# Eleven expert units beside the state space block: side chains at its two ends, list planning inside them, routing decisions in pairs, D on the matrix engine

## The chip, the cores and the metric

The kernel runs on one core of a Trainium2 chip. The metric is the device time of one execution in microseconds (us), the median over several runs. A profile is one further execution, recorded by the hardware profiler; its own time and its span are given below. The engines are TensorE (PE; PEld is its weight load), VectorE (DVE), ScalarE (ACT), GpSimd (POOL) and SyncE (SP, which here only issues DMAs). A line such as L961 is line 961 of the kernel before.

## The reference: what is computed

There are 4096 tokens of 256 float32 values. Three blocks stand one after the other, each with a residual:

```python
x = x + 0.5 * moe(layernorm(x))            # MoE1
x = x + attn(layernorm(x))                 # state space block and a small MLP
x = x + 0.5 * moe(layernorm(x))            # MoE2, the same weights as MoE1

def attn(x):
    x = x + mamba(rmsnorm(x))
    h = square(relu(rmsnorm(x) @ c_fc.T))
    return x + h @ c_proj.T

def mamba(xn):                             # 2 sequences of 2048 tokens
    x_in, z = split(xn @ in_proj.T)        # 512 channels each
    u = silu(causal_conv4(x_in))
    dt_low, B, C = split(u @ x_proj.T)     # 64, 16 and 16 columns
    dt = softplus(dt_low @ dt_proj.T + bias)
    h[t] = h[t-1] * exp(dt[t] * A) + dt[t] * u[t] * B[t]    # 512 channels x 16 states
    y[t] = sum_over_states(h[t] * C[t])
    return ((y + u * D) * silu(z)) @ out_proj.T
```

`moe` picks two of eight experts for each token. Each expert is 256 -> 1024 -> 256 with a ReLU. A token's place in an expert's list is the number of earlier tokens with the same choice; there is a capacity of 1280 places for each choice and expert, and a token beyond it is dropped. So the places of a token depend on the tokens before it and on none after it.

## The kernel before, in words

**Routing.** Tokens are handled in tiles of 128. `route` (L303) normalises a group of n tiles, multiplies with the gate weights, and decides (L374 to L453, many small VectorE operations): the two experts, the gates, and by a running count each token's place in the lists. Then it writes the token numbers into the list tile with a few products against one-hot matrices (`one`, `eqb`, L466, L468, and `ll` on PE, L480 to L488). The normalised rows with their two gates go to the DRAM table `rows`.

**Plan and units.** `store_list` (L495) transposes the list and stores it to DRAM. `plan` (L504) cuts each expert's list into units of 256 places and works out, for all 39 units that could be needed, which list entries a unit takes and which expert's weights. `units` (L570) runs 32 of them: for each unit POOL gathers by indirect DMA two times 128 token numbers (`ids`, L589), the rows (`xb`, L600) and, if the expert changes, its weights (`w`, L609, 2.18 MB); PE transposes the rows (L621), multiplies into the hidden layer (`hp`, L640), ACT adds the bias and takes the ReLU (L645), PE multiplies back (`yp`, L656), VectorE adds the bias and scales by the gate (L660, L661), and POOL scatters with addition into `acc` or `out` (L662). The order is written out by hand: ids five units ahead, rows and weights three ahead. Units past 32 are in a branch that is entered only if the plan needs them. `moe1` (L697) routes all 32 tiles in five groups and then runs its units; `moe2` (L726) finds its routing done by the block before it. Both load three sets of the first expert's weights by SP (L567) beforehand.

**The state space block.** `mamba` (L1095) works on eight chunks of 512 tokens. `recurrence` (L928) has 512 slots: chunk, pair of channel blocks, state, block of the pair. In a slot ACT makes `dA` (L969), POOL `db` (L961; one operation for both blocks of the pair, 128x1024, three tiles in rotation), VectorE the scan `h` (L979) and the product with `ct` (L989), ACT keeps the last state (`st`, L984), and PE sums the products over the states into `y_ps` (L994). SP loads `bt` and `ct`, one row of B and C spread over 128 partitions, one pair ahead into three tiles each. After a pair's 16 states `gate` (L996) adds D times the convolved input (VectorE, L1002) and multiplies by silu(z) (POOL, L1006).

Everything else is a side chain, a generator that yields before each step what the step needs: `chunk_front` (L735: load of `acc`, norms, projections, convolution, dt), `log1p` (L870), `gates` (L893: silu(z)), `chunk_tail` (L1026: output projection, MLP, store of x, and `route` on the chunk's four tiles for MoE2). `Side` (L70) is the planner that interleaves them when the program is built: it counts each engine's use in microseconds (OWN is what a slot takes of each engine) and issues a step when the engines that it needs are no further ahead than BEHIND and its input is not later than EARLY. `until` forces a chain to a mark. What cannot be placed in a slot waits; before the first scan and after the last one the chains run on their own. The engines execute in the order of issue.

Of the kernel before, what the change touches and what calls it, by code (L numbers as in the profile page):

```python
# [17 lines left out]
P = 128  # L18
# [17 lines left out]
NU = K2 * NT // UN  # L36
MU = NU + E - 1
NWB = 3
W_2 = ND * FF
W_B1 = W_2 + NF * D  # L40
W_B2 = W_B1 + NF
# [9 lines left out]
XB = 4  # L51
PR = 2
NP = NC // PR
GROUPS = (4, 4, 8, 8, 8)
# [3 lines left out]
class Need:  # L58
# [4 lines left out]
    def __init__(self, pe=0.0, act=0.0, dve=0.0, pool=0.0, bank=0, free=0, after=None, sets=None):  # L63
        us = {"pe": pe, "act": act, "dve": dve, "pool": pool}
        self.us = {e: t for e, t in us.items() if t}
        self.bank, self.free, self.sets = int(bank), free, sets
        self.after = None if after is None or after[1] < 0 else after


class Side:  # L70
# [6 lines left out]
    OWN = {"dve": 1.8, "act": 0.88, "pe": 0.88, "pool": 1.25}  # L77
# [9 lines left out]
    def begin(self, chain, at=0.0):  # L87
        self.chains.append([chain, None, at])
        self.advance(self.chains[-1])
# [9 lines left out]
    def advance(self, chain):  # L99
        need = next(chain[0], None)  # L100
        while need is not None and not isinstance(need, Need):
            self.begin(need, chain[2])
            need = next(chain[0], None)
        chain[1] = need
        if need is None:
            self.chains.remove(chain)

# [9 lines left out]
    def step(self, chain):  # L117
# [8 lines left out]
        if need.sets:  # L126
            self.mark(need.sets, end)
# [27 lines left out]
    def until(self, mark):  # L155

        while mark[1] >= 0 and mark not in self.marks:
            self.step(min(filter(self.may, self.chains), key=lambda c: self.start(c)[1]))


class Kernel:
# [6 lines left out]
    def setup(self):  # L168
        nc, ins = self.nc, self.ins
        cp = self.ctx.enter_context(self.tc.tile_pool(name="const", bufs=1))  # L170
        self.cpool = self.ctx.enter_context(self.tc.tile_pool(name="count", bufs=2))
        dp = self.ctx.enter_context(self.tc.tile_pool(name="scratch", bufs=1, space=DRAM))
# [32 lines left out]
        self.need = const([P, K2 * CAP // UN], "need")  # L205
        nc.gpsimd.iota(self.need, pattern=[[UN, K2 * CAP // UN]], base=0, channel_multiplier=0,
# [29 lines left out]
        none = const([1, 1], "none_i", I32)  # L236
        nc.gpsimd.memset(none, NT)

# [24 lines left out]
        for c in range(NC):  # L263
            for k in range(DC):
                nc.vector.tensor_scalar_mul(
                    self.taps[:, c, k, :], self.ident, self.half[:, c, k : k + 1]
                )
        self.minus = const([P, 1], "minus")
# [12 lines left out]
        self.rows = dp.tile([NT + 1, RW], F32, tag="rows", name="rows")  # L281
        row = const([1, RW], "none")
        nc.gpsimd.memset(row, 0.0)
        nc.sync.dma_start(out=self.rows[NT:, :], in_=row)
        self.lists = [dp.tile([NULL + 1, 1], I32, tag=f"list{i}", name="lists") for i in range(2)]
        for t in self.lists:
            nc.sync.dma_start(out=t[NULL:, :], in_=none)
# [15 lines left out]
    def route(self, x, t0, pool, bank):  # L303

        nc = self.nc
        n = x.shape[1]
        W, W3, Q = [P, n, E], [P, n, K2], K2 * E
        num = self.exp_m8.unsqueeze(1).to_broadcast(W)

        def t(name, shape=W, dtype=F32, **kw):  # L310
            return pool.tile(shape, dtype, tag=f"r_{name}", name=name, **kw)
# [25 lines left out]
        lg = t("lg")  # L337
        for j0 in range(0, n, 4):
# [22 lines left out]
            for j in range(4):  # L361
# [5 lines left out]
                lg[:, j0 : j0 + 4, :], lq, self.gb.unsqueeze(1).to_broadcast([P, 4, E]), ALU.add  # L367
            )

# [50 lines left out]
        g1 = row[:, :, D]  # L420
        nc.vector.scalar_tensor_tensor(g1, e2, 0.5, rden, ALU.mult, ALU.mult)
        nc.vector.scalar_tensor_tensor(row[:, :, D + 1], rden, 0.5, g1, ALU.mult, ALU.subtract)
# [30 lines left out]
        nc.vector.tensor_tensor(at, at, late, ALU.add)  # L453
        yield Need(dve=1.6)

        WO, WN = [P, n, K2, P], [P, n, K2, E * PB]
# [20 lines left out]
        ll = psum("ll", [P, K2, 2, E * PB])  # L477
# [12 lines left out]
        nc.sync.dma_start(out=self.tiles(self.rows[:NT, :], n)[t0 // n], in_=row)  # L490
# [4 lines left out]
    def store_list(self, pool, ps, to):  # L495

        nc, n = self.nc, K2 * E * PB
        lp = ps.tile([P, P], F32, tag="lists", name="lists")[:n, :]
        nc.tensor.transpose(lp, self.list.rearrange("p c b -> p (c b)"), self.ident)
        lt = pool.tile([P, P], I32, tag="p_list", name="lt")[:n, :]  # L500
        nc.vector.tensor_copy(lt, lp)
        nc.sync.dma_start(out=to[:NULL, :].rearrange("(b p) o -> b (p o)", p=P), in_=lt)

    def plan(self, pool):  # L504

        nc = self.nc
        v = nc.vector
        WE, WB = [P, MU, E], [P, MU, UB]  # L510
        nn = K2 * CAP // UN

        def t(name, shape, dtype=F32):
            return pool.tile(shape, dtype, tag=f"p_{name}", name=name)

        kept, ks = t("kept", [P, K2 * E]), t("ks", [P, E])
        v.tensor_scalar_min(kept, self.count, float(CAP))
        k0 = kept[:, :E]
        v.tensor_tensor(ks, k0, kept[:, E:], ALU.add)
        more, nu, cu, cx = t("more", [P, E, nn]), t("nu", [P, E]), t("cu", [P, E]), t("cx", [P, E])  # L520
        v.tensor_tensor(
            more, ks.unsqueeze(2).to_broadcast([P, E, nn]),
            self.need.unsqueeze(1).to_broadcast([P, E, nn]), ALU.is_gt,
        )
        v.tensor_reduce(nu, more, AX.X, ALU.add)
        v.tensor_tensor_scan(cu, self.ones[:, :E], nu, 0.0, ALU.mult, ALU.add)
        v.tensor_tensor(cx, cu, nu, ALU.subtract)
        past, inn = t("past", WE), t("inn", WE)
        un = self.unum.unsqueeze(2).to_broadcast(WE)
        v.tensor_tensor(past, un, cu.unsqueeze(1).to_broadcast(WE), ALU.is_ge)  # L530
        v.tensor_tensor(inn, un, cx.unsqueeze(1).to_broadcast(WE), ALU.is_ge)
        v.tensor_tensor(inn, inn, past, ALU.subtract)
        eu = t("eu", [P, MU])
        v.tensor_reduce(eu, past, AX.X, ALU.add)

        def of_unit(name, values):
            m, r = t("m", WE), t(name, [P, MU])
            v.tensor_tensor(m, inn, values.unsqueeze(1).to_broadcast(WE), ALU.mult)
            v.tensor_reduce(r, m, AX.X, ALU.add)
            return r.unsqueeze(2).to_broadcast(WB)  # L540

        k0u, ksu, cxu = of_unit("k0u", k0), of_unit("ksu", ks), of_unit("cxu", cx)
        euu = eu.unsqueeze(2).to_broadcast(WB)
        r, m0, m1 = t("r", WB), t("m0", WB), t("m1", WB)
        v.scalar_tensor_tensor(r, cxu, -float(UN), self.upos, ALU.mult, ALU.add)
        v.tensor_tensor(m0, r, k0u, ALU.is_lt)
        v.tensor_tensor(m1, r, ksu, ALU.is_lt)
        at, a1, a0, idx = t("at", WB), t("a1", WB), t("a0", WB), t("idx", WB, I32)
        v.scalar_tensor_tensor(at, euu, float(CAP), r, ALU.mult, ALU.add)
        v.tensor_tensor(at, at, k0u, ALU.subtract)  # L550
        v.scalar_tensor_tensor(a1, at, float(NSLOT - NULL), m1, ALU.add, ALU.mult)
        v.scalar_tensor_tensor(a0, k0u, -float(NSLOT), m0, ALU.add, ALU.mult)
        v.scalar_tensor_tensor(idx, a1, float(NULL), a0, ALU.add, ALU.add)
        same, at2, widx = t("same", [P, MU]), t("at2", [P, MU]), t("widx", [P, MU], I32)
        v.tensor_scalar(same[:, :NWB], eu[:, :NWB], 0.0, None, ALU.is_equal)
        v.tensor_tensor(same[:, NWB:], eu[:, NWB:], eu[:, : MU - NWB], ALU.is_equal)
        v.scalar_tensor_tensor(at2, eu, float(P), self.part, ALU.mult, ALU.add)
        v.scalar_tensor_tensor(widx, same, SKIP, at2, ALU.mult, ALU.add)
        nunits = t("nunits", [1, 1], I32)
        v.tensor_copy(nunits, cu[0:1, E - 1 : E])  # L560
        return idx, m0, widx, nunits

    def first_expert(self, pool):

        w = [pool.tile([P, WW], F32, tag=f"w{i}", name=f"w{i}") for i in range(NWB)]
        for t in w:
            self.nc.sync.dma_start(out=t, in_=self.ins["expert"][:P, :])  # L567
        return w

    def units(self, lo, hi, todo, w, lists, acc, pool, ps):  # L570

        nc = self.nc
        idx, m0, widx, _ = todo
        ids, xb, xT, gate = {}, {}, {}, {}

        def params(u):
            wu = w[u % NWB]
            return (
                wu[:, :W_2].rearrange("p (k f) -> p k f", k=ND),
                wu[:, W_2:W_B1].rearrange("p (f d) -> p f d", f=NF),  # L580
                wu[:, W_B1:W_B2], wu[:, W_B2:],
            )

        def fetch_ids(u):
            if u >= hi:
                return
            ids[u] = pool.tile([P, UB], I32, tag="ids", name="ids", bufs=8)
            for j in range(UB):
                nc.gpsimd.indirect_dma_start(  # L589
# [597 lines left out]
```

## Time and profile before

| | |
|---|---|
| time, median of three runs | 2442.43 us (2440.75 to 2444.05) |
| profiled execution: its own time, its span | 2459.16 us, 2457.4 us |
| busy share of the span | PE 83%, DVE 56%, ACT 42%, POOL 59% |
| first unit's first matmul L640, MoE1 and MoE2 | at 117.9 and 1983.4 us |
| last matmul of MoE1 | at 584.1 us |
| first scan, end of the last scan | at 667.4 and 1893.2 us |
| one bt load, one rows store, median | 3.6 us, 6.5 us |

The profile's page gives the busy time of each engine, the span in slices, the costliest groups of instructions and the DMA issues. A group's row has its line, engine, operation, what it writes and reads, its number, its busy time, the mean ns of one, and the idle time just before it with what ended that. A row of waits names who waited for whom, the sum in us, how often, and the longest. The windows view gives each engine's busy time in a stretch, PE's granted clock as a share of full speed, the DMA engines' busy share and GB/s.

### The profile page before, as it was taken

Reading aid. Unit: us, or ns where it says so; the run is one execution under the profiler, and the core shown is the slowest. Engines: PE = TensorE matmul, PEld = TensorE weight load, DVE = VectorE, ACT = ScalarE, POOL = GpSimd, SP = SyncE. Lnnn points to the kernel's source line nnn. Section 1 sums busy time; section 2 is a strip of 40 time slices with the busy share of each in tenths; the row PEclk is TensorE's granted clock in tenths of the full one; section 3 lists DMA queues with packets and bytes.
Section 4 is the critical chain, followed back from the end, with each engine's and each line's share of the span. In section 5 each row is a group of like instructions: output and inputs, shape, how many; then the busy total and the mean of one; then the engine's idle time right before and its main releaser. Section 6 shows DMA issues by size and latency. Waiting matters only on the chain. (4 is left out here: it accounts for less than half of the span.)

```text
span 2457.4 us, 23707 instructions
## 1 busy us (share of the span) xinstructions
PE 2051.3 (83%) x7196; PEld 1296.4 (53%) x7196; DVE 1386.9 (56%) x2358; ACT 1029.3 (42%) x2307; POOL 1441.5 (59%) x1145
## 2 busy tenths in 40 slices
PE   3499999997687977979889698798686469999998
PEld 1288888885232433424334243243232258888887
DVE  5611111111298989989999899899998301111111
ACT  3122222222467675665756557557343212222222
POOL 2355555642478776675866767668554155556553
PEclk7699999998799988989989899798787779999999
DMA  8145454461133433334434334334342225454463
GB/s 312 62 139 143 117 172 113 114 180 18 57 123 127 121 120 110 121 96 130 142 100 129 102 121 137 94 121 120 111 127 75 108 82 168 121 146 125 131 183 97
DMA packets 141791, 302.00 MB, mean 123 GB/s; under 512 B 24447, under 2 KB 65174, under 8 KB 135638
## 3 DMA queue, kind: packets, MB, share of 16 engines
q1 hardware_dynamic: 103766, 176.50, 23.0%
q0 software_dynamic: 37888, 123.88, 18.2%
q8 instruction: 62, 1.02, 0.2%
q14 instruction: 75, 0.61, 0.1%
HBM read 318.85 MB, written 34.23 MB: 144 GB/s over the span
## 5 line engine op out<-in xcount | busy, mean ns | idle before, releaser
L994 PE MATMUL y_ps<-hc,ident 128*128 128x512 f32 x1024 | 588.8, 676 | 212.3 <-DVE hc L989 200.3
L961 POOL TENSOR_TENSOR db<-dtu,bt 128x1024 f32<-128x1024 f32 x256 | 601.7, 2358 | 207.1 <-DVE h L979 173.8
L645 ACT ACTIVATE h<-hp,w 128x256 f32<-128x256 f32 x512 | 215.0, 471 | 779.3 <-issue 501.7
L979 DVE TENSOR_TENSOR_SCAN h<-dA,st,db 128x512 f32<-128x512 f32 x384 | 494.6, 1288 | 32.3 <-ACT dA L969 3.8
L656 PE MATMUL yp<-w,h 128*128 128x256 f32 x2048 | 457.4, 382 | 10.1 <-issue 10.1
L994 PEld LDWEIGHTS y_ps<-hc,ident 128*128 128x128 f32 x1024 | 184.1, 202 | 531.9 <-DVE hc L989 399.9
L640 PE MATMUL hp<-xbT,w 128*128 128x256 f32 x2048 | 457.5, 382 | 1.6 <-DVE xbT L625 1.6
L640 PEld LDWEIGHTS hp<-xbT,w 128*128 128x128 f32 x2048 | 392.4, 192 | 56.6 <-DVE xbT L625 2.4
L656 PEld LDWEIGHTS yp<-w,h 128*128 128x128 f32 x2048 | 387.1, 192 | 61.7 <-issue 10.9
L969 ACT ACTIVATE dA<-dt,A 128x512 f32<-128x512 f32 x512 | 357.4, 699 | 0.3
L989 DVE TENSOR_TENSOR hc<-h,ct 128x512 f32<-128x512 f32 x512 | 345.1, 674 | 4.7 <-ACT st L984 4.7
L625 DVE COPY xbT<-tp 128x512 f32<-128x512 f32 x64 | 44.3, 692 | 463.6 <-PE tp L621 383.9
L984 ACT COPY st<-h 128x1 f32<-128x1 f32 x512 | 80.7, 158 | 402.9 <-DVE h L979 401.1
L660 DVE TENSOR_TENSOR y<-yp,w 128x256 f32<-128x256 f32 x128 | 54.4, 425 | 340.9 <-PE yp L656 340.9
L662 POOL DMA_INDIRECT acc<-y,ids x64 | 102.5, 1602 | 165.6 <-PE hp L640 76.9
L662 POOL DMA_INDIRECT out<-y,ids x64 | 102.2, 1597 | 165.5 <-DVE y L661 72.1
L979 DVE TENSOR_TENSOR_SCAN h<-dA,db 128x512 f32<-128x512 f32 x128 | 157.1, 1228 | 31.6 <-POOL db L961 17.9
L589 POOL DMA_INDIRECT ids<-lists,idx x128 | 128.5, 1004 | 70.8 <-issue 70.8
L600 POOL DMA_INDIRECT xb<-rows,ids x128 | 130.7, 1021 | 39.0 <-issue 39.0
L909 PE MATMUL in_ps<-rT,w_in 128*128 128x512 f32 x256 | 127.6, 624 | 7.0 <-ACT xpad L794 5.6
L801 PE MATMUL cv_ps<-xpad,taps 128*128 128x512 f32 x256 | 122.2, 603 | 0.1
L909 PEld LDWEIGHTS in_ps<-rT,w_in 128*128 128x128 f32 x256 | 50.2, 200 | 72.9 <-issue 48.1
(199 smaller groups left out, 1944.8 us busy)
## 6 DMA issues: line engine op xcount, KB each, us to landing
bt<-bc SPq DMA_DIRECT2D x256, 256.0 KB, 3.6
ct<-bc SPq DMA_DIRECT2D x256, 256.0 KB, 3.4
w<-in_expert SPq DMA_DIRECT2D x6, 2180.0 KB, 12.8
rows<-row SPq DMA_DIRECT2D x10, 516.0 KB, 6.5
x<-in_x SPq DMA_DIRECT2D x8, 512.0 KB, 8.8
acc<-x SPq DMA_DIRECT2D x8, 512.0 KB, 7.6
x<-acc SPq DMA_DIRECT2D x8, 512.0 KB, 4.9
out<-x SPq DMA_DIRECT2D x8, 512.0 KB, 3.6
```

Of the source, the lines that this page charges most:

```text
L589: nc.gpsimd.indirect_dma_start(out=ids[u][:, j : j + 1], out_offset=None, in_=lists[:, :], in_offset=bass.IndirectOffsetOnAxis(ap=idx[:, u ...
L600: nc.gpsimd.indirect_dma_start(out=xb[u][:, j, :], out_offset=None, in_=self.rows[:, :], in_offset=bass.IndirectOffsetOnAxis(ap=ids[u][:, ...
L640: nc.tensor.matmul(hp[:, q, :], lhsT=w1[:, k, (f + q) * P : (f + q + 1) * P], rhs=xT[u][:, k, :], start=(k == 0), stop=(k == ND - 1),)
L645: nc.scalar.activation(h[:, f + q, :], hp[:, q, :], AF.Relu, bias=b1[:, f + q : f + q + 1])
L656: nc.tensor.matmul(yp, lhsT=h[:, f, j * P : (j + 1) * P], rhs=w2[:, f, :], start=(f == 0), stop=(f == NF - 1),)
L662: nc.gpsimd.indirect_dma_start(out=acc[:, :], out_offset=bass.IndirectOffsetOnAxis(ap=ids[u][:, j : j + 1], axis=0), in_=y[:, j, :], in_of ...
L909: self.nc.tensor.matmul(mp, lhsT=self.w_in[:, k, m * P : (m + 1) * P], rhs=rT[:, k, :], start=(k == 0), stop=(k == ND - 1),)
L961: nc.gpsimd.tensor_tensor(db[n], chunks[i]["dtu"][c // PR], bt[n].unsqueeze(1).to_broadcast(WP), ALU.mult)
L969: nc.scalar.activation(dA[k], chunks[i]["dt"][c], AF.Exp, scale=self.A[:, c, s : s + 1])
L979: nc.vector.tensor_tensor_scan(h[k], dA.pop(k), db[k // PR][:, k % PR, :], chunks[i - 1]["state"][:, c, s : s + 1] if i % (T // TC) else 0 ...
L989: nc.vector.tensor_tensor(hc, h.pop(k), ct[k // PR], ALU.mult)
L994: nc.tensor.matmul(y[c], lhsT=self.ident, rhs=hc, start=(s == 0), stop=(s == DS - 1))
```

## The change

- **Units moved.** MoE1's loop runs 28 units (NU_A). Its plan cuts each expert's list twice, into units that hold tokens of the first half of the sequence and, after all of those, units of the second half alone. The last four (NU_B) run inside `mamba`, in a side chain `beside`, at slots -96, -64, -32 and 0; the load of chunk 4 waits for them. After chunk 3 a plan of the first half of MoE2's lists is made in the chain (`plan_half`); seven full units (NU_C) from it run from slot 448 on. `plan_rest` plans what is left, in the chain after the last chunk, and begins its ids and rows. MoE2's loop runs 25 units (NU_D).
- **Their data.** The expert weights are two tensors (W1 and b1; W2 and b2), gathered separately. The side units have one tile for each (`wa`, `wb`). Rows of the first four chunks go to two tables. SP loads one set of first weights instead of three.
- **Decisions in pairs.** In the block `route` only makes logits and stores rows for an even chunk; the odd one decides for eight tiles at once. Lists are still written per chunk.
- **D on PE.** The accumulation of `y_ps` starts with a matmul of the convolved input by a diagonal matrix `skip`. `gate` is one VectorE product.
- **Buffers.** To make room: `bt` and `ct` 3 -> 2, `db` one tile of 128x512 per slot (4, made three slots ahead), `zs` and `dt` 6 -> 4, `dtu` 3 -> 2, `xc` 8 -> 6, `x` 4 -> 1 (loaded again as `xt` for the tail), `hc` 4 -> 5. The planner's OWN for VectorE is 1.95 instead of 1.8; chains get ranks.

The core of the diff:

```diff
+NU_A, NU_B, NU_C, NU_D = 28, 4, 7, 25
...
-    OWN = {"dve": 1.8, "act": 0.88, "pe": 0.88, "pool": 1.25}
+    OWN = {"dve": 1.95, "act": 0.88, "pe": 0.0, "pool": 1.27}
...
+    def spread_units(self, feed, m0, acc, last, pool, name, slots, known):
...
+        for u, slot in enumerate(slots):
+            yield Need(after=("slot", slot))
+            if u == 0:
+                yield from turn(0)
...
+            for f in range(0, NF, 2):
+                lone = self.lone
+                yield Need(pe=1.8, bank=not lone, after=at("wa", u))
...
+                self.into_hidden(hp, f, w1, xT[u])
...
+            for j in range(UB):
+                yield Need(pe=3.6, bank=j == 0 and not lone, after=at("wb", u))
...
+                self.from_hidden(yp[:, j, :], j, w2, h)
...
+            yield put(u, y)
+            if u + 1 < n:
+                yield Need(pool=1.0, sets=(name + "wb", u + 1), late=9.0)
+                feed.params_of(u + 1, wb)
...
-        def drive(n):
-            if n < len(pairs):
...
-                db[n] = sp.tile(WP, F32, tag="db", name="db", bufs=3)
-                nc.gpsimd.tensor_tensor(
-                    db[n], chunks[i]["dtu"][c // PR], bt[n].unsqueeze(1).to_broadcast(WP), ALU.mult
-                )
+        def drive(k):
+            if k < len(order):
...
+                db[k] = sp.tile(W1, F32, tag="db", name="db", bufs=4)
+                nc.gpsimd.tensor_tensor(db[k], chunks[i]["dtu"][c // PR][:, q, :], bt[n], ALU.mult)
...
             if s == 0:
                 y[c] = pools["yps"].tile(W1, F32, tag="y", name="y_ps")
-            nc.tensor.matmul(y[c], lhsT=self.ident, rhs=hc, start=(s == 0), stop=(s == DS - 1))
+                nc.tensor.matmul(
+                    y[c], lhsT=self.skip[:, c, :], rhs=chunks[i]["xc"][c], start=True, stop=False
+                )
...
+            nc.tensor.matmul(y[c], lhsT=self.ident, rhs=hc.pop(k), start=False, stop=(s == DS - 1))
...
-            nc.vector.scalar_tensor_tensor(
-                yc, ch["xc"][c], self.chan[:, c, DC + 1 : DC + 2], y[c], ALU.mult, ALU.add
-            )
             side.until(("z", NC * i + c))
-            nc.gpsimd.tensor_tensor(yc, yc, ch["zs"][c], ALU.mult)
+            nc.vector.tensor_tensor(yc, y[c], ch["zs"][c], ALU.mult)
...
+        if i % 2 == 0:
+            self.pair = {}
+        yield from self.route(x, i * NJ, pool, lambda tag: (ps, "mm"), to, self.pair)
         yield Need(sets=("routed", i))
+        if i == NCHUNK // 2 - 1:
+            yield self.plan_half(pools["exp"])
+        if i == NCHUNK - 1:
+            yield from self.plan_rest(pools)
...
+    def beside(self, pools):
+
+        chunk = NC * DS
+        slots = [chunk * (u - 3) // 2 for u in range(NU_B)]
...
+        slots = [chunk * (NCHUNK - 1) + 16 * u for u in range(NU_C)]
```

## The prediction, made before the result was known

> **What bounds the kernel now.** I began with the busy shares on the page and the costliest groups, then cut the span into its stages by the windows view, then read the waits inside each stage. The windows give core 0's stretch, its length, and the busy time of each engine, PE's clock, DMA share and GB/s:
>
> ```profile
> 142.30:584.10 441.80, 441.77 (x2106) 388.67 (x2104) 76.81 (x214) 104.13 (x248) 241.61 (x201) 1.00 0.49 136
> 584.10:667.40 83.30, 45.27 (x96) 18.52 (x96) 9.65 (x26) 29.06 (x49) 22.40 (x41) 0.77 0.11 33
> 667.40:1893.20 1225.80, 1003.10 (x2426) 428.20 (x2426) 1126.36 (x1499) 737.48 (x1648) 858.21 (x591) 0.91 0.39 118
> 1893.20:1990.00 96.80, 43.47 (x146) 26.84 (x146) 23.22 (x87) 17.68 (x39) 22.61 (x25) 0.70 0.23 87
> 1990.00:2457.40 467.40, 453.17 (x2152) 398.16 (x2150) 79.53 (x221) 105.81 (x252) 251.80 (x211) 0.99 0.48 135
> ```
>
> Both expert loops are PE from end to end (441.77 of 441.80). The timeline shows one unit every 14.25 us there. The recurrence between them is VectorE: 1126 of 1226 us, PE 82%. Two open ends, 83 us before the first scan and 97 us after the last, have every engine half idle or worse: a chain of small steps. So PE work taken out of a loop is worth its whole time, and costs less at the ends than it weighs, but there it stands in line with the chain's own matmuls.
>
> VectorE's groups inside the recurrence:
>
> ```profile
> L979 DVE TENSOR_TENSOR_SCAN h<-dA,st,db 128x512 f32<-128x512 f32 x384 | 494.6, 1288 | 32.3 <-ACT dA L969 3.8 <-ACT st L984 0.5 <-DVE hc L989 0.5
> L989 DVE TENSOR_TENSOR hc<-h,ct 128x512 f32<-128x512 f32 x510 | 343.8, 674 | 4.7 <-ACT st L984 4.7
> L1002 DVE SCALAR_TENSOR_TENSOR yc<-xc,chan,y_ps 128x512 f32<-128x512 f32 x30 | 22.1, 736 | 1.2 <-PE y_ps L994 1.2
> L385 DVE SCALAR_TENSOR_TENSOR key<-oh,key 128x32 f32<-128x32 bf16 x7 | 7.6, 1089 | 0.0
> L374 DVE TENSOR_REDUCE top<-lg 128x4 f32<-128x32 f32 x7 | 1.3, 184 | 0.2
> ```
>
> A slot (scan 1.29, product 0.67) is 1.99 us with its gap, 1.92 where no state comes in: 128 x 1.925 + 384 x 1.99 = 1011 us. The other 215 are side work and waits. The last two rows are route's: on 128x32 one operation takes 184 ns and another 1089, so operations are the price, not elements. All rows of the decision (L374 to L453) sum to 81.4 us over seven chunks, 11.6 each.
>
> **Part by part**, against the profiled execution's span of 2457.4 us (its own time 2459.16; the median shown is 2442.43, so 0.7% lies between; I carry the difference over unchanged).
>
> *Start of MoE1.* Three weight loads stand in SP's queue ahead of the first row store, and the routing of the second group stands behind that store:
>
> ```profile
> DVE lg L366 <- PE lq L362: 22.4, 4, 15.8
> ```
>
> One load is left there: 2.18 MB of 6.54 that took 21 us is 7 us, so about 14 go (bounds 0 and 15.8). The plan grows: 7.9 us of VectorE now; 39 units x 16 half-expert columns instead of 8, and eight quantities of 39 x 64 elements, each one product and one sum of about 2.6 us: 19.4, +11.5 (bounds +5 and +16). Net **-2.5**, bounds -10 and +10.
>
> *MoE1 loop.* 31 further units become 27: 4 x 14.25 = **-57**. Two weight gathers a unit instead of one add about 1.3 us of POOL, which is busy 242 of 442; without that cover PE would wait 7 us for a late set.
>
> *First open end.* Two units and half a hidden layer are placed there, some 2.3 x 14.25 = 33 us of PE, among 45 us of the chain's own, in 83.3 us. 38 are free; the steps alternate (projection, taps, gate, projection), so a batch of 1.8 to 3.6 us is in the way about every second time. Bounds 0 (all in the holes) and +38 (all in line, with a weight wait). I take **+15**. The row shows a clock of 0.77, and a pass of 512 columns took 0.85 us after idling against 0.43 at full clock. The Trainium skill ("TensorE: Matmul & The Clock Gate", Why this matters for your kernels) says that gaps over about 3 us drop the clock; filling them would make 45.3 us at 0.77 into 35, and the term +5.
>
> *Recurrence.* Decision: three runs on eight tiles (about 12.5 each) for seven on four: 81.4 - 37.5 = -44 (bounds -30 and -50). One list step fewer: -4. Gate 0.68 for 0.736, 30 times: -1.7. D on PE is 32 matmuls of two passes of 0.43, 27 us, beside PE's 223 free; POOL's product behind it (1.27 x 30) goes. Waits for x now loaded early: -8. Added: plan of the first half after chunk 3, some 45 small operations of 0.2 to 0.3 us and more beside POOL, +15 (10 to 25); copies and adds of four units of experts, about 10 x 0.69 = +7. Then new stalls, which no row shows. bt has two tiles for three, db four single ones for three pairs:
>
> ```profile
> POOL db L961 <- DVE h L979: 173.8, 93, 7.2
> POOL db L961 <- DMA bt<-bc: 25.9, 9, 4.5
> ```
>
> POOL runs far ahead now, waiting for VectorE. Two bt tiles serve four slots, 7.96 us, and each is refilled once both products (2.36) are done: a load may take 5.6 us for nothing, and its median is 3.6. A half set of weights beside it (1.1 MB, 3.5 us at 312 GB/s) makes one 7.1: 1.5 us late, 14 times, less what db's lead of three slots hides. In the first and last chunk PE is asked for about 120 of 130 us. I take +10, bounds 0 and +60. Together **-25** (-45 to +35). The Trainium skill ("DMA: Bandwidth & Descriptors", Issuing engines are not separate DMA queues) speaks against the change: gathers from POOL and loads from SP share the same 16 engines, so an idle POOL queue is no spare bandwidth; taken whole, that is 14 x 1.5 = 21 of stalls for my 10.
>
> *Second open end.* Four units less a hidden layer's start stand among row, decision and plan. From the last scan to the list it is 58.5 us; on the path I add 18 (five batches of 3.6), and 4 for the decision on eight tiles, and take off 6 for the clock (43.5 us busy at 0.70 would be 30 at 1.00; half of the 13 lies on the path). From the list to the first matmul it is 31.7, of which
>
> ```profile
> POOL ids L589 <- issue: 25.1, 12, 21.7
> ```
>
> 13 us are the plan's finished indices waiting for a list store that stood behind three weight loads. Now one load is ahead, which went long before; but the plan on 39 units lengthens, the last unit's output weights are gathered behind the new plan's ids on POOL, and its 16 output passes precede unit 0 on PE: 40. So 90.2 becomes 114.5: **+24** (bounds -5 and +45).
>
> *MoE2 loop.* 32 to 25 units: **-99.75**.
>
> Sum: -2.5 - 57 + 15 - 25 + 24 - 99.75 = -145: span 2312, on the median 2442.4 - 145 = **2297 us**.
>
> **Rivals.** *The ends swallow the units:* both ends have about half of PE free and the clock rises, so their terms are 0 and +5 instead of +15 and +24: 2263. Against it: PE executes in order, and an expert batch can't be set aside when a projection becomes ready. *The recurrence stutters:* thinner buffers, POOL's gathers (7.8 us a unit by 241.6/31) between db's and PE's two crowded chunks cost 50 to 60 instead of 10: 2342. For it: db's lead falls from up to five slots to three. Against: 174 us of POOL's idleness. *It is slower:* one mechanism, the bt ring becoming the pace of all slots. Each microsecond over 5.6 costs one per four slots, 128 in all; the gain of 145 is gone when the mean load takes 5.6 + 145/128 = 6.7 us for the whole recurrence. At 7.0 the time is 2476. Against: DMA share 0.39 there and a median of 3.6; weights pass only in the two end chunks. *It doesn't do what it says:* if the routed counts needed more than 28 + 4 or 7 + 25 units, a branch would run 11 and 14 more, 25 x 14.25 = +356. The counts of this input, worked out from the reference's routing, need 31 or 32 units with 19 of the first half, and 11 full first-half units where 7 are used, so it stays shut.
>
> **Numbers.** Forecast (2275 to 2325) 0.52; ends swallow (2250 to 2275) 0.13; stutter (2325 to 2365) 0.20; worse stutter, still faster (2365 to 2437) 0.09; within 0.2%, about what a measurement can tell from no change, 0.01; slower, by bt's ring or the branch, 0.05. The range 2255 to 2365 leaves out 0.15 above and some 0.03 below. Faster 0.94, same 0.01, slower 0.05.
>
> **What would show it.** MoE loops still 14.25 us a unit, 27 and 24 after the first; first scan near 623 us; recurrence near 1200 long with VectorE's decision rows x3 and near 12.5 us a run; POOL's waits on bt under 40 us; last scan to MoE2's first matmul near 114. The prediction is wrong if the bt row's median passes 5.6 us, if scans wait for db or hc's matmuls for over 60 us in the end chunks, or if either open end grows by more than its bound.

## The result, and the profile after

The change made the kernel no faster but 0.3% slower: 2450.14 us against 2441.39 (medians of ten runs each, side by side), a ratio of 1.0031 with a 95% interval of 1.0021 to 1.0040. The forecast was 2297 us. Eleven units of 14.25 us left the loops and about 165 us came back.

The windows of the changed kernel, cut at the same places as before (stretch, length, busy time of PE, PEld, DVE, ACT and POOL, PE's clock, DMA share, GB/s):

```profile
116.00:553.10 437.10, 409.85 (x1900) 353.43 (x1900) 69.18 (x193) 94.04 (x224) 254.82 (x221) 0.99 0.57 171
553.10:664.70 111.60, 79.32 (x249) 47.92 (x248) 13.04 (x32) 38.07 (x72) 43.78 (x65) 0.86 0.27 76
664.70:814.00 149.30, 126.42 (x324) 60.30 (x324) 125.88 (x149) 87.09 (x194) 121.68 (x114) 0.95 0.55 141
814.00:1770.00 956.00, 820.01 (x2027) 359.77 (x2026) 850.11 (x1133) 574.19 (x1290) 670.56 (x647) 0.92 0.49 124
1770.00:1918.70 148.70, 132.00 (x439) 79.70 (x440) 121.19 (x146) 81.10 (x195) 111.64 (x100) 0.94 0.57 149
1918.70:2049.60 130.90, 99.98 (x416) 76.94 (x414) 38.78 (x121) 32.75 (x77) 55.27 (x58) 0.87 0.29 78
2049.60:2451.40 401.80, 364.08 (x1696) 313.49 (x1696) 62.54 (x174) 83.98 (x200) 223.76 (x191) 0.98 0.51 148
```

Look at PE in the first and the last row: 410 of 437 and 364 of 402. The loops have holes now; before, PE had none after the first unit. The recurrence is rows three to five, 1254 us.

A correction to the profile of before: its two loops had 7.4 and 7.3 us more at their first unit (24.6 and 23.8 us from one unit's first matmul to the next) than the same loops show in the run with two bt tiles below (17.1 and 16.5). That is 15 of the 17 us by which the profiled execution lay over the median. The table takes it off. Each stage is from one profile; the changed kernel and the first four experiments have the same code in the recurrence, and there it took 1249.1 to 1255.6 us, so a difference of less than 7 us in it says little.

| stage | before | forecast of the change | measured change |
|---|---|---|---|
| to MoE1's first matmul | 117.9 | -2.5 | -1.9 |
| MoE1 loop | 458.8 | -57 | -21.7 |
| first open end | 83.4 | +15 | +28.2 |
| recurrence | 1226.0 | -25 | +28.1 |
| second open end | 89.9 | +24 | +41.0 |
| MoE2 loop | 466.7 | -99.75 | -64.9 |
| sum | | -145 | +8.8 |

So the forecast missed by 70 us in the loops, 53 in the recurrence and 30 at the ends. (A slip in the text above: `ct` has four tiles in both kernels; only `bt` goes from three to two.)

**The loops.** Here is one unit in the middle of MoE1's loop of the changed kernel, from its timeline (start, length, engine, line, operation; in brackets the idle time before it and what ended that):

```profile
306.19 1.63 POOL L757 DMA_INDIRECT acc<-y,ids  x1 [0.30 <-issue]
...
313.66 1.56 POOL L757 DMA_INDIRECT acc<-y,ids  x1 [5.84 <-issue]
...
315.53 1.06 POOL L197 DMA_INDIRECT xb<-rows,ids  x1 [0.30 <-PE hp L836]
316.89 1.04 POOL L197 DMA_INDIRECT xb<-rows,ids  x1 [0.30 <-issue]
...
318.24 0.99 POOL L197 DMA_INDIRECT w<-in_expert_in,widx  x1 [0.30 <-issue]
318.53 0.14 PEld L775 LDWEIGHTS tp<-ident,xb 128*128 128x128 f32 x1 [2.01 <-issue]
318.56 0.30 PE L775 MATMUL tp<-ident,xb 128*128 128x128 f32 x1 [1.64 <-DMA xb<-rows,ids]
319.54 1.00 POOL L197 DMA_INDIRECT w<-in_expert_out,widx  x1 [0.30 <-issue]
...
323.45 1.63 POOL L757 DMA_INDIRECT acc<-y,ids  x1 [0.30 <-issue]
```

From one first scatter to the next, POOL took 17.3 us, over 14.25, and PE's transposes waited for rows gathered only 2 us earlier. The lead of three units was used up. The largest hole in the round, 5.84 us, stands before the second scatter into `acc`, which may start only when the first has landed. The same wait in the waits view, MoE1's loop:

```profile
POOL acc L757 <- DMA acc<-y,ids: 71.1, 17, 5.2
```

The kernel before has this hole in every unit too, about 3.0 us long, but the view gives most of it another name:

```profile
POOL acc L662 <- PE hp L640: 76.9, 25, 4.3
POOL acc L662 <- DMA acc<-y,ids: 13.3, 4, 3.5
```

In POOL's timeline the waits of the first row, too, all stand before second scatters. A wait is put down to the semaphore that came last by the profile, and the profile of before has no time of landing for these scatters.

After the first unit, eight more still come every 14.2 to 14.3 us, because rows and weights are fetched three units ahead; then that lead is used up, and the rest come every 15.8 on average, save the last, which comes 24.3 us after the one before it. Ahead of its rows POOL had queued the first weights of the side units behind a set of its own, and the hole before the next second scatter grew to 8.1 us:

```profile
523.56 1.57 POOL L757 DMA_INDIRECT acc<-y,ids  x1 [8.13 <-issue]
528.46 0.45 PE L775 MATMUL tp<-ident,xb 128*128 128x128 f32 x1 [6.53 <-DMA xb<-rows,ids]
```

**The recurrence.** VectorE's groups that answer to those shown of before:

```profile
L1384 DVE TENSOR_TENSOR_SCAN h<-dA,st,db 128x512 f32<-128x512 f32 x384 | 494.3, 1287 | 58.7 <-POOL db L1368 25.7 <-ACT dA L1374 4.9 <-DVE hc L1394 0.5
L1394 DVE TENSOR_TENSOR hc<-h,ct 128x512 f32<-128x512 f32 x511 | 344.0, 673 | 13.5 <-ACT st L1389 13.2
L1414 DVE TENSOR_TENSOR yc<-y_ps,zs 128x512 f32<-128x512 f32 x30 | 20.3, 676 | 1.2 <-PE y_ps L1405 1.2
L496 DVE SCALAR_TENSOR_TENSOR key<-oh,key 128x64 f32<-128x64 bf16 x3 | 3.1, 1040 | 0.0
L485 DVE TENSOR_REDUCE top<-lg 128x8 f32<-128x64 f32 x3 | 0.7, 220 | 0.1
```

The busy part went as forecast: the last two rows are the decision on eight tiles, three times instead of seven, at nearly the same price each (1040 for 1089 ns, 220 for 184). VectorE is busy 1097 us, 29 less. But its idle time went from 99 to 157. What ended it, in the waits of the recurrence, and POOL's side of it:

```profile
DVE h L1384 <- POOL db L1368: 57.5, 34, 21.8
DVE zs L1309 <- ACT tz L1306: 13.8, 20, 2.2
DVE v L1463 <- PE out_ps L1458: 13.5, 13, 1.9
DVE hc L1394 <- ACT st L1389: 13.2, 11, 2.7
...
POOL db L1368 <- DMA bt<-bc: 76.0, 60, 3.6
```

21.8 of the first row lie ahead of the first scan. The other 36 are new: before, no scan after the first waited for db. The row of bt was 25.9 and 9 times.

Why a bt load of 3.8 us holds POOL up: with two tiles a load can go out only when POOL has used the pair before the last. For 18 of the waits the trace has both ends of the load: 16 of these loads were issued 0.03 us after that pair's second db ended, and the median one took 3.8 us. By then POOL, catching up after side work, had made the next pair in 2.7 us (median) and stood waiting; over all 60, for 76.0 / 60 = 1.27 us.

### The profile page after: what moved, and what is told of

Read it like the earlier page. It is cut to its first block, busy times and chain, and to the rows that moved or that the text cites. A ratio compares the mean times of both kernels' runs of the same rounds, so it can differ in the third digit from the quotient of the medians.

```text
span 2451.4 us, 24322 instructions
## 1 busy us (share of the span) xinstructions
PE 2076.0 (85%) x7253; PEld 1310.9 (53%) x7253; DVE 1358.1 (55%) x2284; ACT 1023.0 (42%) x2315; POOL 1512.6 (62%) x1461
## 5 line engine op out<-in xcount | busy, mean ns | idle before, releaser
L1368 POOL TENSOR_TENSOR db<-dtu,bt 128x512 f32<-128x512 f32 x512 | 646.9, 1291 | 211.1 <-DVE h L1384 122.3
L1405 PE MATMUL y_ps<-hc,ident 128*128 128x512 f32 x1024 | 567.7, 657 | 146.1 <-DVE hc L1394 145.5
L794 ACT ACTIVATE h<-hp,w 128x256 f32<-128x256 f32 x424 | 178.0, 471 | 672.4 <-PE hp L836 603.2
L836 PE MATMUL hp<-xbT,w 128*128 128x256 f32 x1696 | 377.4, 381 | 1.7 <-DVE xbT L779 1.7
L843 PE MATMUL yp<-w,h 128*128 128x256 f32 x1696 | 378.3, 382 | 0.0
L836 PEld LDWEIGHTS hp<-xbT,w 128*128 128x128 f32 x1696 | 323.8, 191 | 46.8 <-DVE xbT L779 2.4
L843 PEld LDWEIGHTS yp<-w,h 128*128 128x128 f32 x1696 | 320.9, 192 | 42.2
L757 POOL DMA_INDIRECT out<-y,ids x50 | 79.7, 1595 | 121.4 <-DMA out<-y,ids 63.0
L836 PE MATMUL e_hp<-e_xT,wa 128*128 128x256 f32 x352 | 93.3, 416 | 24.0 <-DVE e_xT L890 8.3
L775 PE MATMUL tp<-ident,xb 128*128 128x128 f32 x212 | 42.0, 292 | 72.1 <-DMA xb<-rows,ids 70.6
```

The source lines that it names most:

```text
L757: self.nc.gpsimd.indirect_dma_start(out=dst, out_offset=bass.IndirectOffsetOnAxis(ap=ids, axis=0), in_=y, in_offset=None, bounds_check=las ...
L794: nc.scalar.activation(h[:, f + q, :], hp[:, q, :], AF.Relu, bias=b1[:, f + q : f + q + 1])
L836: self.nc.tensor.matmul(hp[:, q, :], lhsT=w1[:, k, (f + q) * P : (f + q + 1) * P], rhs=xT[:, k, :], start=(k == 0), stop=(k == ND - 1),)
L843: self.nc.tensor.matmul(yp, lhsT=h[:, f, j * P : (j + 1) * P], rhs=w2[:, f, :], start=(f == 0), stop=(f == NF - 1),)
L1368: nc.gpsimd.tensor_tensor(db[k], chunks[i]["dtu"][c // PR][:, q, :], bt[n], ALU.mult)
L1405: nc.tensor.matmul(y[c], lhsT=self.ident, rhs=hc.pop(k), start=False, stop=(s == DS - 1))
```

## The experiments

Two theories stood at the start for the loops (POOL's count of DMAs, or the landing of scatters behind weights), with the bytes moved as a rival. For the recurrence: thinner rings, or the crowd of the units' own work. Ratios are to runs of the kernel before beside each series, which took 2440 to 2457 us; small differences between series are better read from the times and the stages. Kernels that leave work out ran once.

### One weight gather per unit

```diff
-        parts = [to] if n < WW else [to[:, :W_2], to[:, W_2:]]
-        for a in parts:
-            src = self.expert[a.shape[1] != W_2]
-            self.gather(a, src, self.widx[:, u : u + 1], E * P - 1)
+        src = self.expert[{W_2: 0, WW - W_2: 1, WW: 2}[n]]
+        self.gather(to, src, self.widx[:, u : u + 1], E * P - 1)
```

> The two expert loops fetch a unit's weights with one gather (as before) instead of two; the order rows, weights, ids stays. In the changed kernel a unit takes 14.25 us for the first eight units and 15.7 after, and I hold that POOL's own round is what paces it: two scatters of 1.6, the wait of the second for the first to land, and six gathers of 1.3. Theory count (the eighth DMA is what overfills the round): the round loses 1.3, a unit goes to about 14.4, both loops together and the wait before the block lose 60 to 75 us, about 2380. Theory landing (scatters land later because the weights now stand right ahead of them in POOL's queue): the round loses the same 1.3 but the landing stays at 4 to 6 us: about -50, 2395. Theory bytes (26 weight fetches instead of 21 keep the DMA engines busy): no change, 2445.

Measured: 2430.9 us, ratio 0.9937 (0.9915 to 0.9960). MoE1's loop took 436.9 us (437.1 with two gathers), MoE2's 382.1 (401.8). One DMA less did not help the first loop at all; count alone is not it. Landing's own number, 2395, was missed too: the DMA saved 1.3 us, but the hole before the second scatter grew by as much (the table below).

### Weights ahead of the rows

```diff
-                feed.rows_of(u)
                 feed.params_of(u, w[u % NWB])
+                feed.rows_of(u)
```

> Still two weight gathers a unit in the loops, but they are issued ahead of the rows, as before, so two more DMAs stand between the weights and the next scatter. Theory count: no change, 2445 (15.7 us a unit stays). Theory landing: the second scatter's wait falls from 4 to 6 us back to 3.1, a unit goes to 14.3 to 14.8 us, the loops lose 45 to 75: about 2385. Theory bytes: no change.

Measured: 2407.3 us, ratio 0.9839 (0.9805 to 0.9873). Loops 416.8 and 378.6. Swapping two lines gave back 43 us, all of it in the loops: just under the 45 to 75 that landing expects, and far from the nothing that count and bytes expect.

### Both

> One gather and weights first: the loop's DMAs stand as before the change. Theories count and landing: 14.25 us a unit throughout, both loops -72 and the wait for the last scatters of MoE1 -7: about 2370. Theory bytes: no change, because the 26 fetches in 28 units stay.

Measured: 2377.9 us, ratio 0.9719 (0.9686 to 0.9751). Loops 401.5 and 365.6, every unit after the first at 14.2 to 14.3. The weights are all fetched as in the changed kernel (from 150 to 520 us POOL's queue moved 68.0 MB, and 64.4 there), so bytes as such are out. Of the 7 us expected at the last scatters of MoE1, 2.5 came. The waits of POOL in MoE1's loop now read:

```profile
POOL acc L755 <- PE hp L834: 55.9, 18, 4.3
POOL acc L755 <- DVE y L804: 35.1, 20, 7.7
...
POOL acc L755 <- DMA acc<-y,ids: 13.7, 4, 3.9
```

POOL is ahead again. The first row is the second scatters' hole under PE's name, back at 3.1 us each; the second row is mostly first scatters waiting for VectorE's products, which in the changed kernel they hardly did.

### No weight bytes

```diff
-        v.tensor_tensor(same[:, nwb:], eu[:, nwb:], eu[:, : n - nwb], ALU.is_equal)
+        prev = eu[:, nwb:] if nwb == NWB else eu[:, : n - nwb]
+        v.tensor_tensor(same[:, nwb:], eu[:, nwb:], prev, ALU.is_equal)
```

> Leaves out the weights of all loop units after the third (each keeps whatever set lies in its tile): the two gathers are issued as in the changed kernel but with indices out of bounds, so they move nothing. Theory count: still 15 to 15.7 us a unit, since all eight DMAs are issued. Theory landing and theory bytes: 14.25 us a unit, about 2370. Against e2 it tells the two apart: landing expects e2 to gain too, bytes doesn't.

Measured: the total, 2625 us, says nothing: MoE1's changed output routes MoE2 differently, and its loop grew to 604 us. MoE1's loop answers: after the second unit 14.2 to 14.3 us each but for the last (16.1), with all eight DMAs issued. Together with the run of two swapped lines, this leaves landing as the larger part; the DMA count is what still parts those two lines (416.8 and 378.6) from both repairs (401.5 and 365.6).

The two parts of POOL's round in MoE1's loop, medians from 150 to 540 us:

| kernel | first to second scatter | second to next first | whole round |
|---|---|---|---|
| before: one gather, weights first | 4.66 | 9.59 | 14.25 |
| changed: two gathers, rows first | 5.84 | 9.81 | 15.65 |
| one gather, rows first | 7.27 | 8.49 | 15.77 |
| two gathers, weights first | 4.68 | 9.79 | 14.45 |
| one gather, weights first | 4.70 | 9.55 | 14.25 |
| two gathers that move nothing | 4.63 | 9.80 | 14.46 |

The order costs 1.2 to 2.6 us (first column, the third row has all 2.2 MB right ahead of the ids and the scatter). The eighth DMA costs 1.3 (9.81 against 8.49, where POOL never waits for others). Before the change the round had 14.25 - 4.66 - 8.49 = 1.1 us to spare; either part alone overdraws it. The last row does so by 0.2 us a unit, which the lead of three units covered.

### Three bt tiles

```diff
-                bt[n] = bcp.tile(W1, F32, tag="bt", name="bt")
+                bt[n] = bcp.tile(W1, F32, tag="bt", name="bt", bufs=3)
...
-            t = hc[k] = sp.tile(W1, F32, tag="hc", name="hc", bufs=5)
+            t = hc[k] = sp.tile(W1, F32, tag="hc", name="hc", bufs=4)
```

> The changed kernel with three bt tiles again and four hc tiles instead of five to make room. In the changed kernel the recurrence has 157 us of VectorE's idle time against 99 before, of which 36 after the first scan wait for db, and POOL waits 76 us (60 times) for bt against 26 (9). Theory ring (two bt tiles hold POOL up): POOL's waits on bt fall under 30 and scans lose 25 to 35 us of waits, recurrence about 1222, time about 2418. Rival crowd (POOL and PE are crowded by the units' work in the end chunks): bt's waits fall but the recurrence loses under 10 us, 2440.

Measured: 2435.5 us, ratio 0.9975 (0.9964 to 0.9987), against 1.0031 unchanged. Recurrence 1242.0, 12 less. The ring's part is real, between the two theories and less than half of what the ring's gave, although its waits fell from 76 us to 23:

```profile
POOL db L1368 <- DMA bt<-bc: 23.0, 14, 4.0
```

### Without the side units

```diff
-                side.begin(self.beside(pools), rank=4)
```

> Leaves out the eleven side units (their gathers, products and scatters), so their tokens miss those experts; all else stays, the plans too. Theory: first open end back near 90 us (111.6 now; 83.3 before, about 7 of the growth is the last scatters of MoE1 landing late and stays), second open end about 95 (131 now), end chunks freed. Recurrence: if the stalls are the units' crowd, 1254 goes to about 1210; if the thinner buffers, it stays at 1230 or more because the six chunks between have no units.

(The waits for these units go with them.) Measured: 2356.8 us. Open ends 92.4 and 97.7, recurrence 1223.6, between the two expectations. So the eleven units cost 19 and 33 us at the ends and 30 in the recurrence, of which VectorE's own work is only 6 (1097.2 to 1090.9): 24 are stalls. MoE2's loop was 13 us shorter too, but in the other runs without units only 2 to 12.

### Without the side units, three bt tiles

> Leaves out the side units and has three bt tiles, four hc. With both causes gone the recurrence should stand at what VectorE's busy time (about 1091) and the idle time of before (99) give: 1190. If it stays over 1215, something else of the change stalls it: zs and dt on four tiles, db on single tiles, or D's matmuls on PE.

Measured: 2348.6 us, recurrence 1214.4. That is 24 over the 1190 and just under the 1215 from which something else had to be at work: something else was left.

### The kernel before with two bt tiles

```diff
-                bt[n] = bcp.tile(W1, F32, tag="bt", name="bt")
+                bt[n] = bcp.tile(W1, F32, tag="bt", name="bt", bufs=2)
```

> The kernel before with two bt tiles for three, nothing else. Theory ring: POOL's waits on bt go from 26 us to 60 or more, but db there is made for pairs up to five slots ahead, so only part reaches the scans: +5 to +25 us, about 2455. If the ring is harmless: 2441.

Measured: 2448.3 us, ratio 1.0025 (1.0009 to 1.0041), recurrence 1232.0, +6, at the lower end of what the ring's theory expected. No scan after the first waited for db there. POOL's waits on bt were 44 us, not 60.

### Without the side units, wide rings, and the planner's old cost

```diff
-XC = 6
+XC = 8
...
-            yield Need(pe=0.9, bank=1, after=("scan", NP * i + pair - 2))
+            yield Need(pe=0.9, bank=1, after=("scan", NP * i + pair - 3))
...
-            ey = ch["dt"][c] = pool.tile([P, TC], F32, tag="dt", name="dt", bufs=4)
+            ey = ch["dt"][c] = pool.tile([P, TC], F32, tag="dt", name="dt", bufs=6)
```

and likewise `dtu` to three, `zs` to six; the second kernel also sets OWN for VectorE back to 1.8.

> Leaves out the side units, as the two runs without them did, with three bt tiles, and gives zs and dt six tiles again, dtu three, xc eight, with the planner's conditions for them as before the change. Without this the recurrence was 1214 us, with 124 of VectorE's idle time against 99 before. Theory buffers: the waits for tz, db and out_ps are the chains held back by four-tile rings; recurrence near 1190. Rival planner (OWN for VectorE of 1.95 instead of 1.8 makes the planner issue side steps before their inputs are ready): stays above 1208.

> Leaves out the side units; wide buffers as in the run beside it and the planner's OWN for VectorE back at 1.8. Theory planner: 15 to 25 us less recurrence than with 1.95. Theory buffers: within 5 us of it.

Measured: 2339.3 and 2348.1 us; recurrence 1204.2 and 1217.4. The wide rings took 10 us (1214.4 without them), less than half of what their theory gave; with the planner's old cost it was 13 longer, not shorter. The planner theory falls for these kernels, as far as one run of each can say.

### Repaired loops with three bt tiles, and with the old cost

> The changed kernel, all work done, with one weight gather per loop unit ahead of the rows (which gave 2378) and three bt tiles with four hc (which took 12 us off the recurrence). If the two are independent: 2378 - 10 = 2366, ratio to the kernel before 0.969. If the freed loops only move the wait: no better than 2375.

> The same with the planner's OWN for VectorE at 1.8 as before the change. Theory planner: recurrence 10 to 25 us shorter, 2345 to 2355. Theory buffers: within 5 us of 2366; if 1.95 was right for slots with the units' load, some us longer.

Measured: 2366.2 us, ratio 0.9698 (0.9668 to 0.9729), and 2367.2, 0.9701 (0.9676 to 0.9726). The time is the one forecast, but that the two repairs simply add up is not shown: the ratio moved only from 0.9719 to 0.9698, intervals that overlap, and the recurrence from 1249.1 to 1244.3 where the third bt tile alone had given 12. With OWN at 1.8 the recurrence was 12 us shorter (1232.3) and the second open end 6 longer (136.6): no gain in sum, and here the planner's cost does work in the recurrence, other than without units. Why it turns round stays open.

### db by pairs, and a longer lead

```diff
-                db[k] = sp.tile(W1, F32, tag="db", name="db", bufs=4)
+                db[k] = sp.tile(W1, F32, tag="db", name="db", bufs=5)
...
-            t = hc[k] = sp.tile(W1, F32, tag="hc", name="hc", bufs=4)
+            t = hc[k] = sp.tile(W1, F32, tag="hc", name="hc", bufs=3)
...
-            drive(k + 3)
+            drive(k + 4)
```

is the edit of the second kernel against its neighbour; the first makes db as the kernel before does.

> Leaves out the side units. Wide buffers and three bt tiles as in the run without units that took 1204 us in the recurrence, and db made by pairs again (one 128x1024 operation, three tiles, four to five slots ahead). There scans still waited 28 us for db after the first one, against none before the change. Theory lead: these waits go and the recurrence falls to 1175 to 1188. Rival: POOL's blocks of 2.4 us hurt as much as the lead helps, within 5 us of 1204; then the rest of the idle time lies with the planner and D on PE.

> All work done: the changed kernel with one weight gather ahead of the rows, three bt tiles, and db five single tiles made four slots ahead, for which hc has three tiles. Its neighbour with four db tiles took 2366, recurrence 1244 with 27 us of scans' waits for db. Theory lead: those waits halve, 2350 to 2356. Rival: three hc tiles make VectorE wait for PE in the crowded end chunks by as much: 2362 to 2375.

Measured: without units 1201.5 for 1204.2, within the rival's 5 us, though the waits for db after the first scan went from 28 to 2. VectorE was busy 1093 instead of 1085, and waited more for ACT. With all work done, 2357.2 us, ratio 0.9605 (0.9583 to 0.9627), the fastest of those that do all the work, recurrence 1231.4 for 1244.3. (The kernel before took 2456.8 us beside it; to the 2441.4 of the first series it would be 0.966.) Its waits:

```profile
DVE zs L1307 <- ACT tz L1304: 16.5, 21, 2.3
...
DVE v L1461 <- PE out_ps L1456: 13.2, 13, 1.9
...
DVE h L1382 <- POOL db L1366: 6.9, 6, 2.0
```

The scans' waits for db fell from 27.2 to 6.9. So the short lead costs some 13 us where units crowd POOL. Without units its price is not shown by itself: making db by pairs changed POOL's blocks and VectorE's busy time as well.

## Why the prediction was wrong, point by point

**The start of MoE1** (-2.5): right, -1.9.

**The loops** (-57 and -99.75; -21.7 and -64.9): this step failed, and it was the largest. I wrote that two gathers a unit "add about 1.3 us of POOL, which is busy 242 of 442". The 1.3 was right; the cover was not. POOL's other 200 us are mostly not free: about 3 us of each unit are the second scatter waiting for the first to land, which is part of POOL's own round. Before, the round filled 13.1 of 14.25 us, so a unit had 1.1 us to spare for the 1.3. POOL's timeline of before showed it, as holes on a queue that runs in order (in the waits view they are put down to PE), and I read them as reserve. I also never looked at the order of the gathers: the diff puts rows ahead of weights, which leaves only two small gathers between 2.2 MB and the next scatter, and the landing grew with it. Two swapped lines gave 43 us, both repairs 72. Some 10 of MoE1's 36 are the last unit behind the side units' first weights.

The Trainium skill ("DMA: Bandwidth & Descriptors", Rules for kernel authors) says to wait for an accumulating DMA's semaphore before another access of the same bytes. The kernel does, and the rounds above show its price: 4.63 us from one scatter to the next with no weights on their way, 7.27 behind a full set. No run here leaves the wait out.

**The first open end** (+15; +28.2): the units' part was near, 19 by the run without them. The other 9 I had not counted: with the loop's last scatters landing late, and x loaded behind a second copy of itself, the first statistics came 17 us after MoE1's last product instead of 9. With repaired loops it was 14; the second copy's share of the rest is argued, not tried. PE's clock did rise as the ends filled, from 0.77 to 0.86 here and from 0.70 to 0.87 in the second, and both grew nevertheless.

**The recurrence** (-25; +28.1): the mechanism of the gain was right and its size too. The decision gave -49 (forecast -44), lists -7 (-4), the gate -2, the plan +20 (+15), the units +6 (+7), the waits for x -3 (-8). The term for new stalls ("I take +10, bounds 0 and +60") was mis-sized: VectorE's idle time grew by 57. The mechanism that I gave for it, loads made late by weights beside them in the end chunks, did not show: of the bt loads whose landing the trace has (a quarter), none took more than 4.2 us in the first chunk and 5.9 in the last, and 57 of POOL's 76 us of waits on bt lie in the six chunks between, where a single set of weights passes. That "a load may take 5.6 us for nothing" holds only while POOL goes at VectorE's pace; catching up, it made a pair in 2.7. The runs put a price on the parts of the 57: the units' crowd 24, the bt ring 5 to 12 (5 with repaired loops, 9 without units, 12 alone), zs, dt, dtu and xc together 10, db's lead 13 where there are units. These overlap and are no sum, and each is a difference of two profiles; in size they cover it. My rival that stutters named this case, and its price of 50 to 60 was what happened. I gave it less weight because POOL had 174 us of idle time, again a sum over a stage, which does not say whether POOL is ahead when a scan needs it.

**The second open end** (+24; +41.0): the units took 33, where I had put 18 on the path and some of the 8 behind the list. Two holes on PE were not in the account, both from single tiles of the side units, shown in PE's timeline at the end of the chain:

```profile
2024.08 3.78 PE L836 MATMUL e_hp<-e_xT,wa 128*128 128x256 f32 x8 [8.01 <-DVE e_y L944]
2037.39 9.79 PE L843 MATMUL e_yp<-wb,e_h 128*128 128x256 f32 x32 [9.53 <-DMA wb<-in_expert_out,widxc]
2049.62 7.17 PE L836 MATMUL hp<-xbT,w 128*128 128x256 f32 x32 [0.94 <-DVE xbT L779]
```

The first is PE waiting for a bias to be added, which stood on VectorE behind the whole plan (it ran at 2023.3 us, right after the plan's last operation). The second is the last unit's output weights, whose one tile could be refilled only after that; on POOL their gather stood behind four ids gathers and a scatter, and was issued at 2030.1. The rest, 8 us (97.7 without units for 89.9), I put down to pairs and the longer plan; no run shows it.

**The rivals.** The bt ring as the pace of all slots did not come about: bt's median was 3.8 us, far under 5.6. The branch stayed shut: 28 and 25 units ran. By the number the result falls into the class "slower", to which I gave 0.05, but by neither of its two mechanisms: no rival let the loops themselves slow down. Nor did any of the three things come about that I had named as proof of being wrong (bt's median over 5.6 us, scans waiting over 60, an end growing past its bound); of the signs of being right, the first named, loops still at 14.25 us a unit, failed.

## What to carry to other kernels

Before an instruction is put on an engine that "has time", walk one period of its queue in order and add the waits that belong to the queue itself; only what is left is free. Where a serial chain goes through DMA (here scatter, landing, scatter), mind what large transfer is queued ahead of it. And judge a loop by its late periods: a prefetch of three units hid the overload for the first nine units of MoE1's loop.

## What the runs showed of the hardware that was not expected

- A scatter with addition landed later the nearer it stood behind a weight gather on the same queue: the second of a pair followed the first by 4.63 us with no weight bytes ahead, by 4.70 with a set and four small gathers between, and with two small gathers between by 5.84 behind a set in two gathers and 7.27 behind it in one. Indirect gathers whose indices are all out of bounds still cost POOL their full 1.0 us and 0.3 of issue each.
- Splitting POOL's product of 128x1024 into two of 128x512 cost little: 1291 ns each against 2358 for the pair, 44 us of POOL's busy time over the recurrence, and VectorE was busy 8 us less with single ones (1085 against 1093 in the runs without units).
